# A Fourier mix stage on one core: the last row frequency's transform moved into the next group's channel mix, the spectrum's spreading into the first three steps

## The chip, the cores and the metric

The kernel runs on one core of a Trainium2 chip. The metric is the device time of one execution in microseconds (us); before the change it is 7701.62 us, the median of three runs (7698.67 to 7706.48). All data are fp32.

## The reference

The input x has 16 images of 16 channels, 256 by 256 points. Two layers follow each other, each added to its own input. Layer 0 takes a Fourier transform of the normalized input, multiplies it for each pair of frequencies by a 16 by 16 complex matrix that is built from poles and residues, transforms back, and adds a second term that is not touched here. Layer 1 is a chain of small convolutions and a gate.

```
alpha = fft2(group_norm(x))                       # b, i, o (row frequency), x (column frequency)
A  = 1 / (1j * omega1 - weights_pole1)            # per row frequency
Bm = 1 / (1j * omega2 - weights_pole2)            # per column frequency
S  = einsum('ikpq,oikp,xikq->oxik', weights_residue, A, Bm)
output_residue1 = einsum('biox,oxik->bkox', alpha, S)
x1 = ifft2(output_residue1).real
x  = x + x1 + x2                                  # then layer 1
```

The change lies wholly in the stage that makes S, multiplies by it and does the column half of the inverse transform.

## The kernel before

Four functions follow each other: `layer0_forward` (normalization, forward transform, tables), `layer0_mix`, `layer0_back` (row half of the inverse transform and the normalization of layer 1) and `layer1`. `layer0_mix` is the one that changes. In the trace it lies between about 1450 and 3048 us.

Of 256 row frequencies 129 are needed, and they are worked on in 33 groups of four (`NF`, the last with one). For a group g:

- `load_spectrum` (L577 on) brings alpha in four quadrants, each for four of the images, into four buffers `alc`. The loads for the group after the next are issued as soon as a quadrant has been used.
- `expand` (L588) spreads a quadrant over the operand `alb`: it multiplies the same data by four masks (j = 0 to 3), so that in `alb` each of the four row frequencies stands in columns of its own, with zeros for the channels of the others. A quadrant is four pieces of 128 by 1024 elements; ACT does some of the pieces (L593), DVE the others (L595). There is one `alb` only, so a group's spreading comes after the mix of the group before it.
- `poles` (L602 on) makes `lt` on DVE in six products (L609), and `residues` (L617 on) makes S for one output channel k with four matmuls of `lt` and the table `tt` into PSUM (L623). ACT copies even k to the operand `s` (L633), DVE odd k (L631).
- `mix` (L635) is the channel mix: for each of the 256 column frequencies one small matmul, 128 rows, 32 output channels (v and k), 64 columns (four row frequencies by 16 images). Four column frequencies at a time go to the four 32-row quadrants of a PSUM tile `pg`. After every 32 of these matmuls ACT copies the tile to `y` (L649). A matmul of fp32 operands is two instructions in the trace, each with a weight load of its own, so a mix is 512 matmuls and 512 weight loads.
- `turn` (L651) transposes y for one row frequency f: 8 transposes on PE, half of the result copied by DVE (L664), half by ACT (L662) to `yt`.
- `columns` (L667) is the transform back along the columns for one row frequency: 16 matmuls (32 in the trace) of `yt` and the table `ix`, first 8 for the even column frequencies (e = 0), then 8 for the odd ones (e = 1), into two PSUM tiles `ph`. ACT copies the odd part out (L684), DVE makes its sum and difference with the even part (L687, L688), and GpSimd issues the store to `hd` (L692).

The order is written out by hand for all engines: the program keeps each engine's instructions in the order in which the function calls them, and each engine works through its own queue. For group g it is: mix; `poles` for group g+1 and the first two residues; then four steps f = 0 to 3, each with a turn, residues of group g+1, the spreading of quadrant f for group g+1, and the column transform of f. After the last step the next mix begins. It needs all of `alb` and all of `s`.

What a quadrant's pieces are done by, before the change: piece j on ACT if j <= q % 2, else on DVE. So in steps 0 and 2 ACT has one piece and DVE three, and in steps 1 and 3 two and two.

Of the kernel before, what the change touches and what calls it, by code (L numbers as in the profile page):

```python
# [12 lines left out]
AF = mybir.ActivationFunctionType  # L13
ALU = mybir.AluOpType
# [42 lines left out]
def load(nc, pool, src, shape, name):  # L57
    t = pool.tile(shape, F32, tag=name, name=name)
    nc.sync.dma_start(out=t, in_=src)
    return t  # L60
# [487 lines left out]
def layer0_mix(ctx, tc, d, al, hd, tabs):  # L548
# [3 lines left out]
    nc = tc.nc  # L552
# [13 lines left out]
    alb = cp.tile([P, N, 4, nb], F32, name="alb")  # L566
    m4 = load(nc, cp, d["m4"], [P, 4], "m4")
# [9 lines left out]
    def load_spectrum(g, q):  # L577

        t = gp.tile([P, 4, 2, P], F32, tag="alc", name="alc", bufs=4)
        src = al[g].rearrange("v (j h c) b x -> h (v j) c (b x)", h=2, c=8)  # L580
        for h in range(2):
            nc.sync.dma_start(
                out=t[64 * h : 64 * h + 64].rearrange("p b e x -> p (b e x)"),
                in_=src[h, :, :, 4 * q * N : 4 * q * N + 4 * N],
            )
        return t

    def expand(t, q):  # L588

        dst = alb.rearrange("p (x e) j b -> p b e x j", e=2)[:, 4 * q : 4 * q + 4]  # L590
        for j in range(4):
            if j <= q % 2:
                nc.scalar.activation(dst[..., j], t, AF.Copy, scale=m4[:, j : j + 1])  # L593
            else:
                nc.vector.tensor_scalar(dst[..., j], t, m4[:, j : j + 1], None, ALU.mult)  # L595

    def load_poles(g):
        av = ap.tile([P, 32, 4, 3], F32, tag="av", name="av")
        nc.sync.dma_start(out=av.rearrange("p k f l -> p (k f l)"), in_=avd[g])
        return av  # L600

    def poles(av):  # L602


        lt = lp.tile([P, 2, C, 3, 4, 8], F32, tag="lt", name="lt")
        shape = [P, C, 4, 8]
        for h in range(2):
            for plane in range(3):
                nc.vector.tensor_tensor(  # L609
                    lt[:, h, :, plane],  # L610
                    av[:, 16 * h : 16 * h + 16, :, plane].unsqueeze(3).to_broadcast(shape),
                    m8.unsqueeze(1).unsqueeze(2).to_broadcast(shape),
                    ALU.mult,
                )
        return lt

    def residues(lt, s, k0):  # L617

        for k in range(k0, k0 + 2):
            ps = psg.tile([P, 2, N], F32, tag="pg", name="ps")  # L620
            for v in range(2):
                for h in range(2):
                    nc.tensor.matmul(  # L623
                        ps[64 * h : 64 * h + 64, v],
                        lhsT=lt[:, h, k, 1 - v : 3 - v].rearrange("p l f c -> p (l f c)"),
                        rhs=tt[:, h, k],
                        start=True,
                        stop=True,
                    )
            if k % 2:  # L630
                nc.vector.tensor_copy(s[:, :, :, k], ps.rearrange("p v x -> p x v"))  # L631
            else:
                nc.scalar.copy(s[:, :, :, k], ps.rearrange("p v x -> p x v"))  # L633

    def mix(s, y):  # L635

        for x0 in range(0, 64, 8):
            ps = psg.tile([P, 8, 64], F32, tag="pg", name="pg")
            for x in range(8):
                for q in range(4):  # L640
                    i = 4 * (x0 + x) + q
                    nc.tensor.matmul(  # L642
                        ps[32 * q : 32 * q + 32, x],
                        lhsT=s[:, i].rearrange("p v k -> p (v k)"),
                        rhs=alb[:, i].rearrange("p j b -> p (j b)"),
                        start=True,
                        stop=True,
                    )
            nc.scalar.copy(y[:, :, x0 : x0 + 8], ps.rearrange("p x j -> p j x"))  # L649

    def turn(y, f):  # L651

        yt = hp.tile([P, 8, 8, C], F32, tag="yt", name="yt", bufs=2)
        for t0 in range(0, 8, 4):
            pt = pst.tile([P, 4, P], F32, tag="pt", name="pt")
            for t in range(4):
                j = 16 * f + 2 * (t0 + t)
                nc.tensor.transpose(pt[:, t], y[:, j : j + 2].rearrange("p q x -> p (q x)"), ident)
            dst = yt[:, :, t0 : t0 + 4].rearrange("p c t k -> p t c k")
            src = pt.rearrange("p t (c k) -> p t c k", k=C)  # L660
            if t0:
                nc.scalar.copy(dst, src)  # L662
            else:
                nc.vector.tensor_copy(dst, src)  # L664
        return yt

    def columns(g, f, yt):  # L667

        ph = [psh.tile([P, 2, N], F32, tag="ph", name="ph") for q in range(2)]
        for e in range(2):  # L670
            for n, (c, v) in enumerate(((0, 0), (0, 1), (1, 0), (1, 1))):
                i = 2 * (2 * c + e) + v
                for q in range(2):
                    lanes = slice(64 * q, 64 * q + 64)
                    nc.tensor.matmul(  # L675
                        ph[q][:, e],
                        lhsT=yt[lanes, i].rearrange("p t k -> p (t k)"),
                        rhs=ix[lanes, i],
                        start=n == 0,
                        stop=n == 3,  # L680
                    )
        for q in range(2):
            odd = hp.tile([P, 2, P], F32, tag="odd", name="odd", bufs=2)
            nc.scalar.copy(odd, ph[q][:, 1].rearrange("p (v x) -> p v x", v=2))  # L684
            o = hp.tile([P, 2, 2, P], F32, tag="h", name="h", bufs=5)
            even = ph[q][:, 0].rearrange("p (v x) -> p v x", v=2)
            nc.vector.tensor_tensor(o[:, :, 0], even, odd, ALU.add)  # L687
            nc.vector.tensor_tensor(o[:, :, 1], even, odd, ALU.subtract)  # L688
            o = o.rearrange("p v h x -> p v (h x)")
            fy = 4 * g + f  # L690
            if fy % P:
                nc.gpsimd.dma_start(  # L692
                    out=hd[fy, q:nb:2].rearrange("b k v x -> b (k v x)"),
                    in_=o.rearrange("p v x -> p (v x)"),
                )
            else:
                part = fy // P
                nc.gpsimd.dma_start(out=hd[0, q:nb:2, :, part], in_=o[:, 0])

    E = mybir.EngineType  # L700
    with tc.manual_schedule(engines={E.PE, E.Activation, E.DVE, E.Pool}):
        spectrum = [load_spectrum(0, q) for q in range(4)]
        lt = poles(load_poles(0))
        av = load_poles(1)
        s = gp.tile([P, N, 2, C], F32, tag="s", name="s")
        for k0 in range(0, C, 2):
            residues(lt, s, k0)
        for q in range(4):
            expand(spectrum[q], q)
            spectrum[q] = load_spectrum(1, q)  # L710
        for g in range(NF):
            more = g + 1 < NF
            y = gp.tile([P, 64, 64], F32, tag="y", name="y")
            mix(s, y)
            if more:
                lt = poles(av)
                s = gp.tile([P, N, 2, C], F32, tag="s", name="s")
                residues(lt, s, 0)
            for f in range(4 if more else 1):
                yt = turn(y, f)  # L720
                if more:
                    for k0 in range(2 if f == 0 else 4 * f, 4 * f + 4, 2):
                        residues(lt, s, k0)
                    expand(spectrum[f], f)
                    if g + 2 < NF:
                        if f == 0:
                            av = load_poles(g + 2)
                        spectrum[f] = load_spectrum(g + 2, f)
                columns(g, f, yt)


def exponential(nc, pool, y):
# [674 lines left out]
```

## Time and profile before

| Quantity | Value |
|---|---|
| Span of the profiled run | 7700.4 us |
| Mean granted TensorE clock over the span | 0.965 |
| PE (TensorE matmul) busy | 7126.0 us, 93% |
| DVE (VectorE) busy | 4921.2 us, 64% |
| ACT (ScalarE) busy | 3678.6 us, 48% |
| POOL (GpSimd) busy | 2804.5 us, 36% |
| Mix stage, first to last mix | 1479.6 to 3042 us |
| Start of one mix to start of the next, around 2010 us | 47.51 us |

PE is TensorE's matmul part, PEld its weight loads, which overlap with matmuls. The page lists groups of instructions by line, with the busy time, the mean duration in ns, and the idle time of the engine just before them with what ended it. "issue" as the releaser means that the engine waited for nothing that the profile shows. In a timeline, a row gives start, length, engine, line, operation, and in brackets the idle time before it. PEclk is the clock that was granted to TensorE, as a share of full speed. The queue called "instruction" in the list of DMA queues carries the engines' own programs.

Over the stage from 1480 to 3048 us PE is busy for 1382.6 us, DVE for 1007.9 and ACT for 920.9.

### The profile page before, as it was taken

What the parts mean: (1) busy time and instruction counts of PE and PEld (TensorE: products, weight loads), DVE (VectorE), ACT (ScalarE), POOL (GpSimd) and SP (SyncE); (2) the same over time, 40 slices, a digit from 0 to 9 for tenths busy, and PEclk for the clock granted to TensorE, in tenths of its full rate; (3) what the DMA queues carried; (4) which work ended last, traced back from release to release, by engine and by line L of the source; (5) the groups of instructions that cost most, each with busy time, mean ns of one, the idle gap of its engine ahead of it and who ended that gap; (6) DMA issues with size and microseconds to landing.
All of it is one profiled execution on the core that took longest, in us unless ns stands there. A gap on an engine that the chain in (4) does not pass through costs nothing. (4 is left out here: it accounts for less than half of the span.)

```text
span 7700.4 us, 147483 instructions
## 1 busy us (share of the span) xinstructions
PE 7126.0 (93%) x58728; PEld 4107.7 (53%) x58728; DVE 4921.2 (64%) x9184; ACT 3678.6 (48%) x5387; POOL 2804.5 (36%) x3616
## 2 busy tenths in 40 slices
PE   7889999688888988999978999999999999999997
PEld 5778888566666766777733333333333333333332
DVE  8999865366666665666656666666666666666662
ACT  2223333355555554111146656666566655656662
POOL 2334444200000000111135545555554555555552
PEclk9999999899999999999989999999999999999998
DMA  3444444333333333877757788898888898888896
GB/s 99 112 116 121 120 115 108 111 94 94 94 94 94 92 90 121 261 246 245 246 153 216 217 245 248 260 263 251 249 241 251 249 263 256 248 243 251 246 267 205
DMA packets 936290, 1442.20 MB, mean 187 GB/s; under 512 B 91866, under 2 KB 807958, under 8 KB 903606
## 3 DMA queue, kind: packets, MB, share of 16 engines
q1 hardware_dynamic: 792374, 958.51, 44.6%
q0 software_dynamic: 143232, 474.25, 19.4%
q8 instruction: 469, 7.68, 0.4%
q14 instruction: 215, 1.76, 0.1%
HBM read 875.87 MB, written 556.47 MB: 186 GB/s over the span
## 5 line engine op out<-in xcount | busy, mean ns | idle before, releaser
L995 ACT ACTIVATE wide<-c,b 32x512 f32<-32x512 f32 x2176 | 1479.5, 680 | 372.0 <-PE c L946 319.7
L1023 DVE TENSOR_TENSOR t<-pd,r 64x512 f32<-64x512 f32 x1088 | 744.4, 684 | 1321.8 <-PE pd L1015 1298.9
L1026 DVE TENSOR_TENSOR top<-pd,t 32x512 f32<-32x512 f32 x2176 | 1504.3, 691 | 54.8 <-DMA cf<-top 2.3
L1089 PE MATMUL c2ps<-rows,c 128*32 128x512 f32 x12288 | 1393.4, 600 | 20.6 <-ACT e L1098 14.7
L946 PE MATMUL c<-z,w 102*128 102x512 f32 x2048 | 1053.6, 646 | 140.1 <-ACT wide L995 116.3
L1007 POOL COPY wide<-wide 32x1031 f32<-32x1031 f32 (+1 forms) x576 | 570.1, 990 | 1390.1 <-ACT wide L995 1362.7
L1015 PE MATMUL pd<-wide,dw 128*128 128x512 f32 x2048 | 1012.7, 617 | 6.0 <-ACT r L983 3.2
L1089 PEld LDWEIGHTS c2ps<-rows,c 128*32 128x32 f32 x12288 | 388.7, 109 | 992.3 <-issue 885.1
L946 PEld LDWEIGHTS c<-z,w 102*128 102x128 f32 x2048 | 399.2, 197 | 703.8 <-issue 515.3
L1015 PEld LDWEIGHTS pd<-wide,dw 128*128 128x128 f32 x2048 | 376.7, 194 | 626.5 <-issue 458.2
L692 POOL DMA_DIRECT2D hd<-h x254 | 151.9, 598 | 1373.2 <-DVE h L688 1353.2
L631 DVE COPY s<-ps 128x512 f32<-128x512 f32 x264 | 271.4, 1028 | 508.5 <-PE ps L623 487.2
L1008 POOL COPY wide<-wide 32x1031 f32<-32x1031 f32 (+1 forms) x576 | 573.4, 996 | 35.9
L1098 ACT ACTIVATE e<-c2ps,b 128x512 f32<-128x512 f32 x256 | 176.0, 687 | 855.3 <-PE c2ps L1089 852.7
L313 PE MATMUL px<-wxn,u 128*64 128x256 f32 x4224 | 558.7, 385 | 2.1 <-ACT o L320 1.8
L813 PE MATMUL py<-h,iy 128*128 128x256 f32 x2048 | 541.5, 383 | 5.2 <-issue 5.2
L623 PE MATMUL ps<-tt,lt 128*64 128x256 f32 x4224 | 496.1, 385 | 37.9 <-DVE lt L609 37.3
L642 PE MATMUL pg<-alb,s 128*32 128x64 f32 x16896 | 310.6, 240 | 196.3 <-issue 185.2
L675 PE MATMUL ph<-ix,yt 64*128 64x256 f32 x4128 | 480.4, 382 | 0.7 <-ACT yt L662 0.7
L313 PEld LDWEIGHTS px<-wxn,u 128*64 128x64 f32 x4224 | 401.1, 136 | 127.4 <-ACT o L320 5.3
L813 PEld LDWEIGHTS py<-h,iy 128*128 128x128 f32 x2048 | 385.2, 191 | 108.4 <-issue 50.0
L675 PEld LDWEIGHTS ph<-ix,yt 64*128 64x128 f32 x4128 | 389.0, 187 | 89.9 <-issue 49.2
(202 smaller groups left out, 10343.7 us busy)
## 6 DMA issues: line engine op xcount, KB each, us to landing
rows<-cf SPq DMA_DIRECT2D x128, 2176.0 KB
z<-zn SPq DMA_DIRECT2D x768, 256.0 KB
cf<-top POOLq DMA_DIRECT2D x512, 240.0 KB, 7.3
cf<-bot POOLq DMA_DIRECT2D x96, 840.0 KB, 10.4
alc<-al SPq DMA_DIRECT2D x264, 256.0 KB
zn<-zb SPq DMA_DIRECT2D x128, 516.0 KB
o<-zn SPq DMA_DIRECT2D x64, 1032.0 KB
z<-in_x SPq DMA_DIRECT2D x64, 1024.0 KB
```

The source lines that it names most:

```text
L313: nc.tensor.matmul(ps[64 * k : 64 * k + 64, :, h], lhsT=u[:, h, part, g0 + j + k].rearrange("p f c -> p (f c)"), rhs=wxn[:, h, part], star ...
L623: nc.tensor.matmul(ps[64 * h : 64 * h + 64, v], lhsT=lt[:, h, k, 1 - v : 3 - v].rearrange("p l f c -> p (l f c)"), rhs=tt[:, h, k], start= ...
L675: nc.tensor.matmul(ph[q][:, e], lhsT=yt[lanes, i].rearrange("p t k -> p (t k)"), rhs=ix[lanes, i], start=n == 0, stop=n == 3,)
L813: nc.tensor.matmul(py[:, yh], lhsT=iy[:, v, ys], rhs=h[:, k, v], start=v == 0, stop=False)
L946: nc.tensor.matmul(ps[:, q], lhsT=w, rhs=cols[:, 1 - q], start=True, stop=True)
L995: nc.scalar.activation(self.feat[64 - 32 * q : 96 - 32 * q, f, self.groups[g], :H], ps[32 * f : 32 * f + 32, q], AF.Mish, bias=b1[0][32 * ...
L1007: nc.gpsimd.tensor_copy(flat[0:32, f, 1:m], flat[64:96, f, 0 : m - 1])
L1008: nc.gpsimd.tensor_copy(flat[96:128, f, 0 : m - 1], flat[32:64, f, 1:m])
L1015: nc.tensor.matmul(ps, lhsT=dwt if self.tail else dw, rhs=self.feat[:, f, cs, :H], start=True, stop=True,)
L1023: nc.vector.tensor_tensor(t[64:128], ps[:64], self.r[:, cs], ALU.mult)
L1026: nc.vector.tensor_tensor(self.top[32 * f : 32 * f + 32, cs, q], ps[lanes], t[lanes], ALU.add)
L1089: nc.tensor.matmul(ps[32 * j : 32 * j + 32], lhsT=c2[:, blk, dx, :], rhs=t[:, 4 * j + blk : 4 * j + blk + 4, x : x + H], start=(blk, dx) = ...
```

## The change

It has three parts.

1. `columns` becomes a generator that stops between its even and its odd half. For the first three row frequencies of a group it is run to its end at once, as before. For the last one (f = 3) it is handed to the mix of the next group, which calls for the even half before its 25th column position of 64 in each quadrant (x0 = 24), and for the odd half with the evictions before its 49th (x0 = 48). Between the last residues and the mix there is then no transform.
2. The spreading is cut into pieces by a table `spreads`: ACT does two pieces in each of the first three steps and DVE three. In the last step only one piece is left, (3, 3) on DVE, and it stands ahead of that step's residues. In sum ACT has 6 pieces and DVE 10, as before.
3. `poles` for the next group is called before the mix instead of after it, so that its six products stand ahead of the deferred transform's evictions in DVE's queue.

It is for filling the mix with other work of PE, and for letting the mix begin without waiting for the spreading of the last quadrant.

```diff
-    def expand(t, q):
-
-        dst = alb.rearrange("p (x e) j b -> p b e x j", e=2)[:, 4 * q : 4 * q + 4]
-        for j in range(4):
-            if j <= q % 2:
-                nc.scalar.activation(dst[..., j], t, AF.Copy, scale=m4[:, j : j + 1])
-            else:
-                nc.vector.tensor_scalar(dst[..., j], t, m4[:, j : j + 1], None, ALU.mult)
+    def expand(t, q, j, eng):
+
+        dst = alb.rearrange("p (x e) j b -> p b e x j", e=2)[:, 4 * q : 4 * q + 4, :, :, j]
+        if eng is nc.scalar:
+            eng.activation(dst, t, AF.Copy, scale=m4[:, j : j + 1])
+        else:
+            eng.tensor_scalar(dst, t, m4[:, j : j + 1], None, ALU.mult)
+
+
+    spreads = (
+        (((0, 0), (1, 0)), ((0, 1), (0, 2), (0, 3))),
+        (((1, 1), (2, 0)), ((1, 2), (1, 3), (2, 1))),
+        (((3, 0), (3, 1)), ((2, 2), (2, 3), (3, 2))),
+        ((), ((3, 3),)),
+    )
+
+    def spread(spectrum, f):
+        for eng, parts in zip((nc.scalar, nc.vector), spreads[f]):
+            for q, j in parts:
+                expand(spectrum[q], q, j, eng)
...
-    def mix(s, y):
+    def mix(s, y, between):
+
 
         for x0 in range(0, 64, 8):
+            if x0 in (24, 48):
+                next(between, None)
...
         for e in range(2):
+            if e:
+                yield
...
         for q in range(4):
-            expand(spectrum[q], q)
+            spread(spectrum, q)
+        for q in range(4):
             spectrum[q] = load_spectrum(1, q)
+        between = iter(())
         for g in range(NF):
             more = g + 1 < NF
             y = gp.tile([P, 64, 64], F32, tag="y", name="y")
-            mix(s, y)
             if more:
                 lt = poles(av)
+            mix(s, y, between)
+            if more:
                 s = gp.tile([P, N, 2, C], F32, tag="s", name="s")
                 residues(lt, s, 0)
             for f in range(4 if more else 1):
                 yt = turn(y, f)
                 if more:
+                    if f == 3:
+                        spread(spectrum, f)
                     for k0 in range(2 if f == 0 else 4 * f, 4 * f + 4, 2):
                         residues(lt, s, k0)
-                    expand(spectrum[f], f)
+                    if f < 3:
+                        spread(spectrum, f)
...
-                columns(g, f, yt)
+                between = columns(g, f, yt)
+                if f < 3:
+                    for _ in between:
+                        pass
```

## The prediction

> **What bounds the kernel now.** I read the page first. Part 1 has PE at 93% of the span, no other engine over 64%; the slices with the most PE idle after the start lie between 1480 and 3048 us, which is the mix stage. In part 5 its matmuls are the one large PE group with idle time of its own:
>
> ```profile
> L642 PE MATMUL pg<-alb,s 128*32 128x64 f32 x16896 | 310.6, 240 | 196.3 <-issue 185.2
> ```
>
> The waits of PE, cut to 1480 to 3048 us, say that this is nearly all the idle time there, and that almost none of it is for data:
>
> ```profile
> PE pg L642 <- issue: 172.4, 90, 4.8
> PE pg L642 <- ACT alb L593: 9.4, 32, 0.3
> ```
>
> 172.4 us over 33 mixes is 5.2 us each, in 90 pieces, about 2.7 a mix. The columns are total, times, longest. The timeline of PE over one row-frequency group shows where the pieces are:
>
> ```profile
> 2009.51 3.44 PE L642 MATMUL pg<-alb,s 128*32 128x64 f32 x232 [0.29 <-ACT alb L593]
> 2015.41 1.99 PE L642 MATMUL pg<-alb,s 128*32 128x64 f32 x128 [2.46 <-issue]
> 2019.16 1.99 PE L642 MATMUL pg<-alb,s 128*32 128x64 f32 x128 [1.75 <-issue]
> 2022.90 0.54 PE L642 MATMUL pg<-alb,s 128*32 128x64 f32 x24 [1.75 <-issue]
> ...
> 2049.39 3.67 PE L623 MATMUL ps<-tt,lt 128*64 128x256 f32 x32
> 2053.00 3.72 PE L675 MATMUL ph<-ix,yt 64*128 64x256 f32 x32
> 2057.02 2.99 PE L642 MATMUL pg<-alb,s 128*32 128x64 f32 x197 [0.30 <-ACT alb L593]
> ```
>
> A stall comes after every 128 matmuls. Each has its weight load, so that is 256 instructions. The list of DMA queues over 2009.5 to 2023.4 us has three packets on the queue that carries instructions, 16 KB each (0.05 MB), one for each stall:
>
> ```profile
> q8 instruction: 3, 0.05, 1.3%
> ```
>
> So a block of 256 instructions takes PE 1.99 us to use up and 3.74 us (2015.41 to 2019.16) to be replaced: the mix is bound by instruction fetch. The four steps after it use up 128 matmuls in about 14.9 us (32 in 3.72) and never stall. The second cost is the clock. Windows of three mixes and of the inside of one:
>
> ```profile
> 2009.50:2023.50 14.00, 8.03 (x514) 7.46 (x516) 5.03 (x10) 4.54 (x9) 1.20 (x2) 1.00 0.33 93
> 2057.00:2070.50 13.50, 8.02 (x514) 7.45 (x514) 5.03 (x10) 4.56 (x9) 1.20 (x2) 1.00 0.34 96
> 2104.10:2120.50 16.40, 10.35 (x514) 9.70 (x514) 5.03 (x10) 4.54 (x9) 1.20 (x2) 0.79 0.30 80
> ...
> 2110.00:2113.00 3.00, 0.00 (x0) 0.00 (x0) 0.00 (x0) 0.00 (x0) 0.00 (x0) 1.00 0.49 163
> 2113.00:2116.40 3.40, 1.82 (x70) 1.83 (x74) 0.00 (x0) 0.59 (x1) 0.00 (x0) 0.50 0.04 8
> ```
>
> After the stretch column come its length and the busy time of PE, PEld, DVE, ACT, POOL, then the clock. A mix needs 8.03 us of PE at full clock. In the third mix a stall of 4.77 us (2109.8 to 2114.6) is followed by a clock of 0.50, and PE needs 10.35. Over all mixes it is 310.6 / 33 = 9.4 us, 1.4 more than at full clock. The row 2110 to 2113 also shows why that stall is long: data move at 163 GB/s, the fetch comes behind them.
>
> **What the Trainium skill says.** "Runtime: NRT & Kernel Launch", section "Instruction fetch mechanics": the instruction memory is refilled in 16 KiB blocks of 256 instructions, the next fetched while the current one runs; the cost is said to be mostly hidden. The trace agrees on the size (a stall every 128 matmuls with their loads) and not on the cost, 5.2 us a mix. "TensorE: Matmul & The Clock Gate", section "Part 1: The HAM clock gate": PE's clock halves after a free-running window of some 3.4 us in which PE was too idle; the 0.50 after the 4.77 us stall agrees.
>
> **The change, part by part.** It acts at 32 of the 33 mixes (the first has no transform before it).
>
> *Removed between the last residues and the mix:* the 32 transform matmuls of the last step, 3.72 us, and the wait of 0.30, together 4.02 us (2053.00 to 2057.02). What ends the wait now is the spreading on ACT; DVE has its own two spreads there:
>
> ```profile
> 2050.63 0.67 DVE L664 COPY yt<-pt 128x512 f32<-128x512 f32 x1
> 2051.39 1.02 DVE L631 COPY s<-ps 128x512 f32<-128x512 f32 x1
> 2053.12 1.03 DVE L631 COPY s<-ps 128x512 f32<-128x512 f32 x1 [0.71 <-PE ps L623]
> 2054.00 2.58 DVE L595 TENSOR_SCALAR alb<-alc,m 128x1024 f32<-128x1024 f32 x2
> ...
> 2053.07 3.90 ACT L593 ACTIVATE alb<-alc,m 128x1024 f32<-128x1024 f32 x2
> ```
>
> After the change ACT spreads nothing in the last step, and DVE one piece, ahead of its two copies. Two spreads take 2.58 and the mean is 1.39, so one starts 1.19 after the other. The piece starts at 2051.35, the first copy at 2052.55, the second 0.88 later (2053.12 to 2054.00) at 2053.43, ending at 2054.45. The mix can start 0.05 later (ACT ended at 2053.07 + 3.90 = 2056.97, the mix started at 2057.02): 2054.50, or 1.5 us after the residues. Removed: 4.02 - 1.5 = **2.5 us**. This wait for the last copy is new. Behind it in PE's queue stand the mix and, after it, the next steps; ACT's copies of y wait for the mix, and the transposes for those copies. If the moved piece held up nothing it would be 1.2; if DVE ran half a microsecond late, 2.0.
>
> *Moved on ACT and DVE:* the totals stay, 6 and 10 pieces. Each of the first three steps now has ACT 2 and DVE 3. Before, each load stood alone in some step: DVE 3 in the first and third, ACT 2 in the second and fourth. A step lasts 8.28 us (8 transposes, 32 residue and 32 transform matmuls, 1.09 + 3.67 + 3.72 less overlaps). DVE's is 0.76 (copy to yt) + 2 x 0.88 + 3 x 1.19 + 4 x 0.34 (evictions of a transform) = 7.5, ACT's 0.59 + 2 x 1.02 + 3.90 + 0.65 = 7.2, so both still wait for PE within it, and I cost this at nothing. The six pole products on DVE (3.69 us) now come ahead of the last transform's evictions. PE is busy in the mix for 8 us or more before those can start. ACT's two copies of that transform stand ahead of the last two copies of y in its queue, 1.3 us in all (2 x 0.65 at most), and the transposes that need y come only after 16 residue matmuls (1.95 us).
>
> *Added inside the mix:* 32 transform matmuls, 16 after the 192nd and 16 after the 384th of the 512. **+3.7 us**, at 0.116 each.
>
> *Stalls:* a block with 16 transform matmuls takes 112 x 0.0155 + 16 x 0.116 = 3.6 us to use up, against 3.74 to fetch. Undisturbed stalls are then 0.15 there and 1.75 in a plain block. I take the first fetch at 4.3 (1.99 + 2.30, a longer one of the middle kind) since the last quadrant's load still meets it. Where the first block boundary falls beyond the 32nd matmul (three cases of four, as it drifts from mix to mix: 232, 197, 162 above), three blocks end in the mix: 4.3 and two of 3.75, less 3.6 + 3.6 + 1.99, or 2.6 us. Otherwise a fourth, plain one ends there too, and it is about 4.3. Mean 3.0, so 5.2 - 3.0 = **2.2 us** less. Bounds: 2.0 left with no disturbed fetch, 3.8 if fetches are disturbed as often as now.
>
> *Clock:* fewer windows are mostly idle, but a half clock would now also slow the transforms. I take 0.5 us left of 1.4, **0.9 us** less; bounds 0 and 1.2 left.
>
> Sum: -2.5 + 3.7 - 2.2 - 0.9 = -1.9 us, times 32 = -61 us, from 7701.6 to about 7640. The stages after only shift.
>
> **Rivals.** *A, all stalls of disturbed fetches vanish, and the half clock with them:* -2.5 + 3.7 - 3.2 - 1.4 = -3.4, times 32 = -109: 7593. For it: the last transform's stores, which now leave in the early mix beside the loads, move to its end, and the last load starts some 4 us sooner. Against: plain blocks remain, with stalls of 1.75. *B, the fetches stay as disturbed as they are:* stalls 3.8, clock 1.0 left: -2.5 + 3.7 - 1.4 - 0.4 = -0.6: 7682. For it: a fetch of 6.76 us (1.99 + 4.77) stalls a block of either kind. *C, slower:* the fetch does not run ahead under the transforms, so stalls and clock stay and the 3.7 us are simply moved into the mix: -2.5 + 3.7 = +1.2, times 32 = +38: 7740. The same sign results if the denser first three steps make PE wait by more than 0.5 us each. Against it: in the steps, which hold no other PE work than residues, transposes and transforms, PE never stalls for issue, and the block that lies half in the last step and half in the mix passes its end free (its end is at matmul 104, and the first run of 232 goes on over it).
>
> **How the numbers follow.** My forecast 0.50, A 0.22, B 0.16, C 0.12. The forecast, A and most of B lie below 7686 (0.2% faster): 0.83. The rest of B and the milder part of C are within 0.2%: 0.08. Slower: 0.09. The range goes from A's 7593 up to 7695, which takes in B and leaves out C and the tails.
>
> **What would show it.** In the changed profile the mix's first matmul waits about 1.5 us for the last DVE copy of s, not for ACT. The idle time from issue drops from 172 to about 100 us (33 x 3.0), mostly in pieces of 1.75. The mix matmuls average well under 240 ns busy, and the clock of the stage rises. No wait above 0.3 us appears in the first three steps. I am wrong if blocks with transforms in them still stall by over 1 us, if the wait before the mix is over 3 us, or if PE waits for spreads or evictions within a step.

## The result, and the profile after

The changed kernel takes 7630.69 us, the median of four runs (7628.49 to 7635.8), against 7700.15 us for the kernel before. The ratio is 0.9909, with a 95% interval of 0.9892 to 0.9926: 0.9% faster. The forecast was 7640 us with a range of 7593 to 7695.

From the first mix to the last the stage has shrunk from 1548.0 to 1481.3 us in the profiled runs, by 66.7 us. The two profiled spans differ by 66.4, so the other stages have kept their length.

In the page's part 5 and in the full list of groups, the mix's matmuls after the change, and the transforms that now partly lie among them:

```profile
L692 PE MATMUL ph<-ix,yt 64*128 64x256 f32 x4128 | 503.5, 391 | 7.4 <-issue 6.8 <-ACT yt L677 0.7
...
L657 PE MATMUL pg<-alb,s 128*32 128x64 f32 x16896 | 277.2, 222 | 137.0 <-issue 90.5 <-DVE s L643 46.0
```

The mix matmuls are busy for 277.2 us and not 310.6, and their idle time by "issue" is 90.5 and not 185.2. A new item stands beside it, 46.0 us for DVE's copy to `s`. The transforms' busy time has risen by 23.1 us (480.4 before), though their number is the same. Some 9 us of it come from splitting: a run of 32 took 3.72 us, and two runs of 16 take 2.00 us each (rows below), 32 times. The rest is transforms that run at a lower clock.

The waits of PE from 1479.3 to 2960.6 us (total, times, longest; the 12.9 us piece is the wait before the first mix of all, there in both kernels):

```profile
PE pg L657 <- issue: 88.7, 46, 12.9
PE pg L657 <- DVE s L643: 46.0, 32, 1.5
PE ph L692 <- issue: 6.8, 6, 2.9
PE ps L635 <- issue: 3.8, 4, 1.8
```

The 32 waits for DVE are the new wait before the mix, 46.0 / 32 = 1.44 us each, where 1.5 was worked out. The timeline of PE in one group:

```profile
2028.63 3.67 PE L635 MATMUL ps<-tt,lt 128*64 128x256 f32 x32
2033.73 2.89 PE L657 MATMUL pg<-alb,s 128*32 128x64 f32 x192 [1.43 <-DVE s L643]
2036.55 2.00 PE L692 MATMUL ph<-ix,yt 64*128 64x256 f32 x16
2038.47 2.42 PE L657 MATMUL pg<-alb,s 128*32 128x64 f32 x155
2042.45 0.76 PE L657 MATMUL pg<-alb,s 128*32 128x64 f32 x37 [1.55 <-issue]
2043.13 2.00 PE L692 MATMUL ph<-ix,yt 64*128 64x256 f32 x16
2045.06 2.11 PE L657 MATMUL pg<-alb,s 128*32 128x64 f32 x128
```

The mix now follows the residues after 1.43 us. One stall of 1.55 us is left of three. Counting mix and transform matmuls alike, it comes at number 192 + 16 + 155 = 363. One block of 128 earlier is 235, so the block from 235 to 363 is the plain one, which holds no transform. The two blocks that hold 16 transforms end without a stall.

The same can be counted over all 32 mixes with transforms, in blocks of 128 from each stall. 57 blocks hold all 16 matmuls of one half of the transform; after them PE stalls by 0.09 us in the mean, after 2 of them by over 1 us. After the 35 plain blocks that lie wholly in a mix it stalls every time, by 1.91 us in the mean. The 14 blocks that hold only some of the 16 lie between, at 0.71.

Not all mixes are like this. Here is one with a long stall, and the window of the clock behind it:

```profile
1799.64 2.32 PE L657 MATMUL pg<-alb,s 128*32 128x64 f32 x151 [1.44 <-DVE s L643]
1805.40 0.77 PE L657 MATMUL pg<-alb,s 128*32 128x64 f32 x41 [3.44 <-issue]
1806.11 3.29 PE L692 MATMUL ph<-ix,yt 64*128 64x256 f32 x16
```
```profile
1805.50:1808.00 2.50, 2.50 (x53) 2.13 (x54) 0.00 (x0) 0.59 (x1) 0.00 (x0) 0.73 0.05 15
```

A stall of 3.44 us ends a plain block, with 201 GB/s of data moving in it. (In the stall of 1.55 us above nothing moved.) The clock then halves within the window (0.73 on the mean of 2.5 us), and 16 transforms take 3.29 instead of 2.00 us.

The period of a group, cut in three (means over 32 periods of the profiled runs, in us, measured between the starts and ends of PE's instructions; the stalls within the mix take in those before its transforms):

| Part of the period | Before | After |
|---|---|---|
| last residue to the mix's start | 3.95 | 1.44 |
| the mix, with the transforms in it | 14.72 | 15.06 |
| the four steps, up to the last residue | 29.71 | 29.79 |
| sum | 48.38 | 46.29 |
| stalls within the mix | 5.30 | 2.48 |
| stretches of halved clock in the stage, and their time | 26, 116 us | 10, 34 us |

### The profile page after: what moved, and what is told of

The parts are those of the page before. It is cut to its first block, busy times and chain, and to the rows that moved or that the text cites. A ratio compares the mean times of both kernels' runs of the same rounds, so it can differ in the third digit from the quotient of the medians.

```text
span 7634.0 us, 147451 instructions
## 1 busy us (share of the span) xinstructions
PE 7110.6 (93%) x58728; PEld 4078.3 (53%) x58728; DVE 4906.0 (64%) x9184; ACT 3674.3 (48%) x5387; POOL 2832.8 (37%) x3616
## 5 line engine op out<-in xcount | busy, mean ns | idle before, releaser
L709 POOL DMA_DIRECT2D hd<-h x254 | 188.6, 742 | 1281.9 <-DVE h L705 1262.0
L635 PE MATMUL ps<-tt,lt 128*64 128x256 f32 x4224 | 497.0, 385 | 37.8 <-DVE lt L621 34.0
L692 PE MATMUL ph<-ix,yt 64*128 64x256 f32 x4128 | 503.5, 391 | 7.4 <-issue 6.8
L207 PE MATMUL pu<-fy,eo 128*128 128x128 f32 x2048 | 424.7, 291 | 12.0 <-DVE u L224 8.3
L594 DVE TENSOR_SCALAR alb<-alc,m 128x1024 f32<-128x1024 f32 x330 | 418.9, 1394 | 0.0
```

Of the source, the lines that this page charges most:

```text
L635: nc.tensor.matmul(ps[64 * h : 64 * h + 64, v], lhsT=lt[:, h, k, 1 - v : 3 - v].rearrange("p l f c -> p (l f c)"), rhs=tt[:, h, k], start= ...
L692: nc.tensor.matmul(ph[q][:, e], lhsT=yt[lanes, i].rearrange("p t k -> p (t k)"), rhs=ix[lanes, i], start=n == 0, stop=n == 3,)
```

## The experiments

Times are medians. Each ratio is to the kernel before, run on the same chip, with its 95% interval. Two theories were to be told apart at first: the gain comes from filling the fetch's stalls, or from the mix no longer waiting for the spreading.

**Spreading alone.** The transform stays ahead of the mix; the pole products have moved as in the change.

```diff
                 between = columns(g, f, yt)
-                if f < 3:
-                    for _ in between:
-                        pass
+                for _ in between:
+                    pass
```

> The new spreading and the products ahead of the mix, but the last transform stays between the residues and the mix. Theory (the gain comes from filling the instruction fetch's stalls with transforms): the stalls stay near 172 us, only the 0.3 us before each mix goes, so about 7690 us, 8 to 10 below before. Rival (the gain comes from the mix no longer waiting for the spreading): most of the 69 us is kept, 7650 or less.

Measured: 7663.58 us, ratio 0.9954 (0.9939 to 0.9968). That is half of the whole gain, and neither theory had it. The wait shrank as foreseen, from 3.95 to 3.58 us (the transform itself), but the mix too became shorter, from 14.72 to 13.70, with no transform in it. Its stalls are 158 us in sum against 170, and the halved stretches 17 against 26. The timelines of DVE and PE in this kernel show what else has moved:

```profile
2043.51 1.45 DVE L594 TENSOR_SCALAR alb<-alc,m 128x1024 f32<-128x1024 f32 x1
```
```profile
2045.29 3.73 PE L692 MATMUL ph<-ix,yt 64*128 64x256 f32 x32
2048.95 1.27 PE L657 MATMUL pg<-alb,s 128*32 128x64 f32 x76
```

And SyncE's queue, which issues the loads, in the kernel before and in this one:

```profile
2032.97 25.23 SPq L582 DMA_DIRECT2D alc<-al  x8
2032.36 13.87 SPq L582 DMA_DIRECT2D alc<-al  x6
```

The last piece is spread 4 us before the mix begins (2043.51 + 1.45 = 2044.96, the mix at 2048.95), where before the change ACT's last piece ended just as the mix began. The last quadrant's next load waits for these pieces. Before the change its issue ended at 2058.20, 1.2 us after the mix began (2057.02); here it ends at 2046.23, 2.7 us before. So the load had moved too, and a new theory was needed: its data delay the fetches. This is followed up below.

**Deferral alone.** The quadrants are spread as before the change, after each step's residues.

```diff
-        (((0, 0), (1, 0)), ((0, 1), (0, 2), (0, 3))),
-        (((1, 1), (2, 0)), ((1, 2), (1, 3), (2, 1))),
-        (((3, 0), (3, 1)), ((2, 2), (2, 3), (3, 2))),
-        ((), ((3, 3),)),
+        (((0, 0),), ((0, 1), (0, 2), (0, 3))),
+        (((1, 0), (1, 1)), ((1, 2), (1, 3))),
+        (((2, 0),), ((2, 1), (2, 2), (2, 3))),
+        (((3, 0), (3, 1)), ((3, 2), (3, 3))),
...
-                    if f == 3:
-                        spread(spectrum, f)
                     for k0 in range(2 if f == 0 else 4 * f, 4 * f + 4, 2):
                         residues(lt, s, k0)
-                    if f < 3:
-                        spread(spectrum, f)
+                    spread(spectrum, f)
```

> The last transform goes into the next mix, but each quadrant is spread in its own step as before (ACT 1, 2, 1, 2 pieces, DVE 3, 2, 3, 2, after the residues). Theory: the mix waits about 4 us after the residues for ACT's two pieces, so it starts no earlier than before the change, the transforms add 3.7 us to it and take 2.5 us of stalls away, and an idle time of 4 us halves the clock at the start of nearly every mix: about 7750 us, slower than before. Rival (the deferral alone makes the gain, the spreading is a detail): 7630 to 7660 us.

Measured: 7707.16 us, 1.001 (1.0003 to 1.0016). It is no gain, as foreseen, but the loss is 7 us and not 50. The timeline of PE and the windows of one mix show both sides:

```profile
2064.08 4.44 PE L657 MATMUL pg<-alb,s 128*32 128x64 f32 x192 [3.89 <-ACT alb L592]
2068.45 2.00 PE L692 MATMUL ph<-ix,yt 64*128 64x256 f32 x16
```
```profile
2060.30:2064.00 3.70, 0.00 (x0) 0.00 (x0) 3.70 (x4) 3.70 (x3) 0.00 (x0) 1.00 0.62 196
2064.10:2067.30 3.20, 3.20 (x124) 3.20 (x127) 3.02 (x6) 0.59 (x1) 0.00 (x0) 0.50 0.32 92
```

PE idles 3.89 us for ACT, and the clock is 0.50 right after. That much was expected, and all 32 mixes meet the half clock within their first 3.4 us. What I had missed is that a block at half clock lasts nearly as long as a fetch (124 matmuls in 3.20 us in the row above, a fetch every 3.74 us): the stalls fall to 1.05 us a mix, not to 2.8. The fetches themselves do not run ahead during the wait: no packet of PE's instruction queue lies in any of the 32 waits. Of the orders tried, the deferral pays only where the spreading clears the way.

**Both halves in one place.**

```diff
-            if x0 in (24, 48):
-                next(between, None)
+            if x0 == 32:
+                for _ in between:
+                    pass
```

> As the changed kernel, but both halves of the transform run together before the 33rd column position. Theory (each block of 256 instructions has to last as long as a fetch): one block then holds 5.3 us of work against 3.7 to 4.3 of fetching, and one more block than now is plain and stalls by 1.7, so stalls rise by 1.2 to 2 us a mix: 7670 to 7695 us. Rival (any work in the mix hides the stalls, wherever it stands): 7630 us.

Measured: 7655.16 us, 0.9945 (0.993 to 0.996), 24 us more than the change. The place matters, so "any work hides the stalls" falls. Stalls within the mix went from 2.48 to 3.36 us, a rise of 0.9 where I had 1.2 to 2: the sign is right and the size too large.

**The pole products behind the mix.**

```diff
-            if more:
-                lt = poles(av)
             mix(s, y, between)
             if more:
+                lt = poles(av)
                 s = gp.tile([P, N, 2, C], F32, tag="s", name="s")
```

> As the changed kernel, but the six pole products are called after the mix, as before, so they stand behind the deferred transform's evictions on DVE. Theory: they start only when those are done, at about the mix's end, and the first residues wait some 3 us for them: 7720 to 7740 us. Rival (DVE has slack, the order doesn't matter): 7630 us.

Measured: 7769.7 us, 1.0087 (1.007 to 1.0104), slower than before the change by 0.9%. The waits of PE between 1482.5 and 2924 us name it:

```profile
PE ps L635 <- DVE lt L621: 79.8, 55, 1.9
```

The residues wait some 2.8 us a group for `lt` (79.8 us over 28.6 groups of 50.4 us), and 28 stretches of halved clock are back (112.6 us). The loss is larger than I gave. I had left the clock out: 112.6 us at half clock, where the changed kernel has 34, cost up to 39 us more. The third part of the change, which looks like a side issue, is needed.

**Moving the last quadrant's load, first trial.** The load was written after the next mix in the program.

```diff
+                    if f == 0 and g:
+                        spectrum[3] = load_spectrum(g + 1, 3)
...
-                        spectrum[f] = load_spectrum(g + 2, f)
+                        if f < 3:
+                            spectrum[f] = load_spectrum(g + 2, f)
```

> As the changed kernel, but the last quadrant's load for the group after the next is issued after the next mix, at its first step, and no longer at the end of the fourth step, just before the mix. Theory (the stalls over 2 us and the halved clock after them come from fetches that wait behind this load's data): stalls fall from 88 to about 65 us, halved windows from 10 to 3 or fewer, 7580 to 7600 us. Rival (a fetch takes 3.3 to 5.7 us by its own jitter, whatever else moves): stalls and clock as in the changed kernel, 7630 us, give or take 8.

Measured: 7624.99 us, 0.9908 (0.9891 to 0.9924): no change. The trial does not speak against the theory. The loads' queue waits for nothing but free buffers, and no load stands between the third quadrant's and this one, so it started as early as before: its first half is issued 1.8 us before the mix in this trace as in the changed kernel's. Its place in the program did not move the transfer, since nothing ahead of it in its queue waited.

So this run is in effect a second profile of the changed kernel, and it tells how far counts can be trusted: it has 7 stalls over 2.05 us and 6 halved stretches, where the changed kernel's profile has 13 and 10, and the two ratios are the same.

**No loads.** The loop's spectrum loads are left out, and groups 2 to 32 work on the data of group 1.

> As the changed kernel, but the spectrum is not loaded again inside the loop: groups 2 to 32 work on the data of group 1, everything else stays. Theory (data traffic delays the fetches): hardly a stall over 1.8 us in a mix, no halved clock, 7575 to 7595 us. Rival (jitter of the fetch itself): 7630 us.

Measured: 7595.55 us, 0.9869 (0.9849 to 0.9888). That is at the upper edge of what I gave. After the first mix there is no halved clock up to the last one. Two stalls over 2.05 us are left, of 13 in the changed kernel and 7 in the run above. Without the loads the fetches are nearly regular.

**The load held until the mix is nearly over.** GpSimd issues it, and in its queue it stands after the deferred transform's stores.

```diff
-    def load_spectrum(g, q):
+    def load_spectrum(g, q, eng=nc.sync):
...
             mix(s, y, between)
+            if more and g:
+                spectrum[3] = load_spectrum(g + 1, 3, nc.gpsimd)
...
-                        spectrum[f] = load_spectrum(g + 2, f)
+                        if f < 3:
+                            spectrum[f] = load_spectrum(g + 2, f)
```

> As the changed kernel, but the last quadrant's load is issued by GpSimd and stands in its order after the deferred transform's stores, so that it cannot start before the mix is nearly over (the load moved in the earlier trial had nothing to wait for in its queue and started as before). Theory (this load's data make the fetches early in the mix late): the stalls over 2 us and the halved windows go from 13 and 10 to 4 or fewer each, 7595 to 7610 us. Rival (other traffic or the fetch's own jitter): 7625 to 7635 us.

Measured: 7605.11 us, 0.9873 (0.9858 to 0.9888), 26 us below the change. The first 6 us of the 13th mix, in the changed kernel and then in this one (DMA share and GB/s are the last two columns):

```profile
2033.73:2039.73 6.00, 6.00 (x297) 5.44 (x301) 3.38 (x6) 1.85 (x4) 0.00 (x0) 1.00 0.56 180
```
```profile
2029.25:2035.25 6.00, 6.00 (x297) 5.44 (x301) 3.38 (x6) 1.85 (x4) 0.00 (x0) 1.00 0.25 80
```

The waits of PE in this kernel, 1482.5 to 2924 us:

```profile
PE pg L657 <- issue: 55.4, 40, 2.5
PE pg L657 <- DVE s L643: 44.7, 31, 1.5
```

Data traffic in the early mix is down from 180 to 80 GB/s. Stalls over 2.05 us went from 13 to 6, the longest is 2.5, and the halved stretches went from 10 to 6 (20 us). The counts are above the "4 or fewer" I gave, and no lower than in the trial that left the load where it was (7 and 6), so they settle nothing. The time does: it is within what I gave, and its interval lies below those of the changed kernel and of that trial. The mix fell from 15.06 us (14.61 in that trial) to 14.09, and the wait before it is the same.

The changed kernel's trace by itself points the same way. Of the 42 stalls over 0.5 us in its 32 later mixes, 23 have less than 20 GB/s of data in them; these last 1.42 us in the mean and 2.03 at most. All 13 over 2.05 us are among the other 19.

**The same load held in the kernel before**, with nothing else of the change. GpSimd copies one column of the mix's result first, so as to wait for it.

```diff
-    def load_spectrum(g, q):
+    def load_spectrum(g, q, eng=nc.sync):
...
             mix(s, y)
+            if more and g:
+                held = hp.tile([P, 1], F32, tag="held", name="held")
+                nc.gpsimd.tensor_copy(held, y[:, 0, 63:64])
+                spectrum[3] = load_spectrum(g + 1, 3, nc.gpsimd)
...
-                        spectrum[f] = load_spectrum(g + 2, f)
+                        if f < 3:
+                            spectrum[f] = load_spectrum(g + 2, f)
```

> The kernel before, with one edit: the last quadrant's load is issued by GpSimd after a one-column copy of the mix's result, so that it starts after the mix. Nothing is deferred or spread anew. Theory (spreading alone gained 37 us because the last piece done early lets this load move out of the mix): the mix shortens from 14.7 to 13.7 us or less, halved windows from 26 to 17 or fewer, 7660 to 7675 us. Rival (spreading alone gains by engine work that moved, not by the load): 7700 us.

Measured: 7672.11 us, 0.9964 (0.9951 to 0.9977). Moving this load alone takes the mix from 14.72 to 13.82 us and the stretches from 26 to 20, both a little less than I gave. The kernel with spreading alone has 13.70 there. The two gains, 29 and 37 us, differ by about the 0.37 us a group that spreading also takes off the wait (32 x 0.37 = 12). So most of what spreading alone gains can be put down to this load leaving the mix; the sizes agree, though no run shows that they are the same microseconds.

The changed kernel does not have this gain. The loads' queue in it, and then what that queue moves in the first 6 us of the 13th mix, in the kernel before, with spreading alone, and in the changed kernel (packets, MB, share of the DMA engines):

```profile
2012.21 20.93 SPq L582 DMA_DIRECT2D alc<-al  x8
```
```profile
q1 hardware_dynamic: 144, 0.52, 30.3%
q1 hardware_dynamic: 58, 0.20, 10.1%
q1 hardware_dynamic: 288, 0.72, 38.8%
```

Spreading alone leaves 0.20 MB of the load there, of 0.52 before. In the changed kernel the load's issue ends at 2033.14, only 0.6 us before the mix (2033.73), because the mix itself has moved forward. The whole load, 0.5 MB, falls into the mix's first 6 us again, and the poles' load of 0.2 MB with it. The times agree: with the load held in both kernels the change is worth 0.9873 / 0.9964 = 0.9909, the same as with the load held in neither (0.9909; each of these ratios is known to about 0.0015).

**The poles' load held too, and the last residue's copy split** over DVE and ACT, to shorten the wait before the mix.

This is on top of the held load.

```diff
-        nc.sync.dma_start(out=av.rearrange("p k f l -> p (k f l)"), in_=avd[g])
+        (nc.gpsimd if g > 1 else nc.sync).dma_start(out=av.rearrange("p k f l -> p (k f l)"), in_=avd[g])
...
-            if k % 2:
+            if k == C - 1:
+                nc.vector.tensor_copy(s[:, :, 0, k], ps[:, 0])
+                nc.scalar.copy(s[:, :, 1, k], ps[:, 1])
+            elif k % 2:
                 nc.vector.tensor_copy(s[:, :, :, k], ps.rearrange("p v x -> p x v"))
```

> As the run with the held load, and in addition the poles' load is held in the same way and the last residue's copy is split, half on DVE and half on ACT. The wait before the mix should fall from 1.45 to about 1.0 us (the half copy takes some 0.5 us less), 32 times, and the poles' 192 KB leave the mix: 15 to 25 us below the run with the held load, if DVE's last copy is what ends that wait. Rival (the wait is the semaphore's and the queue's own, not the copy's length): no difference.

Measured: 7592.91 us, 0.9855 (0.9839 to 0.9871). The split failed in what it was for. The timeline of ACT before a mix:

```profile
2022.37 1.01 ACT L648 COPY s<-ps 128x512 f32<-128x512 f32 x1 [0.70 <-PE ps L635]
2024.08 0.59 ACT L644 COPY s<-ps 128x256 f32<-128x256 f32 x1 [0.70 <-DVE s L643]
```

ACT's half waits for DVE's half and runs after it, not beside it, so the wait is 1.56 us, longer than before the split. The stretches of halved clock are down to 1.

**The two held loads without the split.** The edit is that of the run before, less its second part.

> As the run with the held load, with the poles' load held too, and without the split copy. In the run that had both, the half copy on ACT waited for the half on DVE and the wait before the mix did not shrink (1.56 us), so the split should have given nothing. If so this run is at 7590 to 7596 us, as that one was; if the split did help after all, at 7605, as with the one held load.

Measured: 7600.08 us, 0.9868 (0.9852 to 0.9885), between the two times I gave. The intervals of this one, of the one with the split and of the one with a single held load overlap. The runs do not say whether the second held load or the split adds anything. What holds is that all three beat the change, by 0.3 to 0.5%.

## Why the prediction was right

*The fetch bounds the mix.* Right. The transforms' place decides (24 us between two places). Blocks that hold 16 of them stall by 0.09 us in the mean where I had 0.15, and plain blocks by 1.91 where I had 1.75. The sign I had named for being wrong, a stall of over 1 us in a block with transforms, does occur, in 2 of the 57 full ones and 4 of the 14 that hold fewer.

*The mix starts 2.5 us sooner.* Right: 3.95 - 1.44 = 2.51. The chain was worked out to end 5.11 us after the last step's residues begin (2049.39 to 2054.50); it took 5.10 (2028.63 to 2033.73). The new wait is for DVE's copy, as named. Deferral alone, where this way is blocked, gained nothing.

*The moved work on ACT and DVE costs nothing.* Right. No step waits for a spread or an eviction. The poles' place, which I had costed at nothing together with it, is free only where the change has put it: behind the mix the products cost 139 us against the changed kernel.

*The stalls, -2.2.* Nearly right. They fell from 5.30 to 2.48 in the mix, and 0.1 a group has appeared just after it (3.8 us by "issue" at L635, over 32), so 2.6 are left where I had 3.0.

*The clock, -0.9.* Right. I had 0.5 us a group left of 1.4. At half clock at most half of a stretch is lost, so the 34 us of halved stretches cost at most 17 us, or 0.5 a group.

*The transforms, +3.7.* A little low. Two runs of 16 take 2.00 us each, not half of 3.72. The 22 mixes that run wholly at full clock last 12.03 us without their stalls; the 7 such mixes before last 8.04. So the term is +4.0.

*The sum.* With +4.0, -2.8 and -0.9 the mix should have grown by 0.3 us; it grew by 0.34. The whole period fell by 2.09 us where I had 1.9. That it is so close is in part luck: the transforms cost 0.3 more than I had, and the stalls fell by 0.5 more.

*The rivals.* C, slower because a fetch does not run ahead under the transforms, fell at once: those blocks hardly stall. B, fetches as disturbed as before, fell too: it had stalls of 3.8 us and 1.0 us of half clock left, and 2.6 and 0.5 are measured. A, that the disturbed stalls vanish altogether, did not come true in this kernel; with the load held the time comes near it, 7605 us with A at 7593. What I had named for A was that the last load starts some 4 us sooner. It does, against the residues of the last step. But the mix starts 2.5 us sooner too, so against the mix it is 1.8, and the load still falls into it, as the term for the first fetch had assumed. That data delay a fetch I had read off a single row (163 GB/s in the stall of 4.77 us); only the runs with the load held or left out test it.

## What to carry to other kernels

Where an engine stalls for "issue" at even counts of instructions, compare the time that a block of 256 takes with the time of one fetch, and give every block enough long instructions to last as long as that; one heavy block beside plain ones was worth less here. Before work is moved into such a stretch, look at what feeds its start and at what the moved work releases in other queues: here one part of the change taken alone gained 37 us, mostly by letting a load leave the stretch, and the other part moved the stretch onto that load again. To hold a transfer out of a stretch, put it behind something that its own queue waits for; a later line in the program did nothing here.

## What the runs showed of the hardware

Instruction fetches come later where data move. In the kernel before, a fetch comes every 3.74 us from block to block in the mix shown first, and after 6.76 us (1.99 and a stall of 4.77) in the one with 163 GB/s of data in that stall. In the changed kernel's trace all 13 stalls over 2.05 us have more than 20 GB/s of data in them, and none of the 23 with less is longer than 2.03 (before the change it is 28 of 49 against 3 of 31). Holding one 0.5 MB load out of the mix is worth 29 us in the kernel before and 26 in the changed one. How the data delay the fetch is not shown.

The TensorE clock goes to half after one stretch of 3.41 us in which PE idled for more than about half of it. By the clock records and PE's instructions, all 26 halved stretches of the mix stage before the change followed one with at least 59% idle, and those of the changed kernel one with 52 to 93%. Over all twelve traces the least idle share that was followed by half clock is 51%, and the largest that was not is 60%; ends of matmuls are modelled, so the limit is not sharper than that. So a stall of 1.75 us (51% of such a stretch), which mostly passes when it is alone, can cost twice when two of them, or a longer one, fall into one such stretch.

Two copies by ACT and DVE from two halves of one PSUM tile into interleaved columns of one operand ran one after the other, ACT waiting 0.70 us for DVE. Whether the program's own ordering or the memory made this wait was not tried.
